# Row sums on ScalarE and a new spread of the fallback's pieces in the first layer of a two-layer kernel

## Chip, cores and metric

One Trainium2 chip, one core of it. The metric is the device time of one launch in microseconds (us). The kernel takes all inputs from HBM and writes the final activations there; float32 throughout, apart from one table of masks.

## The reference

The input `x` has 16 sequences of 256 tokens, 128 features each (4096 tokens). Four blocks follow one another, each as `x = x + block(layernorm(x))`:

```
x = x + L0_attn(layernorm(x))   # linear attention: 32 heads of 4, a decaying state per head, two decays, then an own norm
x = x + L0_ffn(layernorm(x))    # 8 experts, each token to its two best, 1280 places an expert; a dense "fallback" FFN
x = x + L1_attn(layernorm(x))   # gated decay scan
x = x + L1_ffn(layernorm(x))    # two transformer layers with a local window
```

What the change touches lies between the first two. `layernorm` is the usual one,

```
m = mean(x, -1);  v = var(x, -1);  (x - m) / sqrt(v + 1e-5)
```

and the rows that it gives go to the experts and to the fallback network, `gelu(h @ fw1 + fb1) @ fw2 + fb2` with 512 hidden units, whose result stands for a token that an expert had to turn away.

## The kernel before, in words

The 4096 tokens are cut into 8 blocks of 512 (`NB`, `BW`). The first layer is one loop over `t` from -2 to 7 (L796), written out by hand as a software pipeline: in pass `t`, block `t` is scanned, block `t+1` is projected and prepared, block `t-1` is closed, and block `t-2` is normalised for the experts. `do(1, "weigh", cc)` means: step `weigh` of block `t+1`. Each engine runs its instructions in the order in which the loop records them, so a waiting instruction holds up all that stands behind it on its engine. Nothing reorders them.

What one pass does, in the order of the code:

- VectorE (DVE) scans `s` for the two denominators (L505, `s<-beta,phik`). These two scans start a pass in what follows.
- `rotate` for `k` and then for `q` (L448): two projections on TensorE (PE) into PSUM banks `pp`, two products on VectorE, one sum on GpSimd (POOL).
- `add`, `gather`, `den`, `project`, `gates` (PE, with copies on ScalarE, ACT), `share` (a reciprocal on VectorE and a product on POOL), `query`.
- `measure_z`, `sp.sqrt()` and `sp.scales()`: means, variances and scales for the attention's own norm of block `t-1`, and in the same call for the experts' norm of block `t-2`; a `Spread` object has 8 places for them, 0 to 3 for `z` and 4 to 7 for `x`.
- `raised`, `rows_z`, `rows_x`, `rows_n` on ACT; `product`, `shift`, `close` on POOL.
- `value 0` and `value 1` (PE), then `spread_beta 0` (PE, four matmuls into a bank `beta`), `add` of the first decay (PE, `y`), and four rounds of scan, `weigh` (VectorE, `kv<-phik,pp`, reads the bank of `value`) and further `value`s. Between them `turn` (PE `ht`, ACT `hT`), `turn_n` (PE `nt`, ACT `u`) and `logits` (PE `pl`, ACT `lg`).
- `measure_n` (L568): four `bn_stats` and four `bn_aggr` on VectorE over the rows of block `t-1`, which POOL has just finished (L565).
- `spread_beta 1` (PE).

The projections, the transposes, the logits and the fallback's first matmuls share one pool of three PSUM banks (`pp`, L296), which go round in the order of the requests: a matmul into a bank waits until the bank's last reader is done.

Two things run beside. `Route(0, 8)` in pass 4 and `Route(8, 20)` in pass 7 choose experts and places for tokens; their steps are taken one by one with `tick()`, and are mostly small VectorE instructions with a few matmuls (`rt`). And `fallback()` (L731) is cut into pieces, taken with `fill(n)`: for each block, four pieces `inward` (one matmul of 512 columns into a bank `fh`, then one gelu on ACT, L742) and four pieces `outward` (four matmuls of 128 columns each into a bank `fo`; the last one's copy `u<-fo` on ACT, L752). Three blocks (`EARLY`) are done inside the loop, two more after it. Before the change passes 5, 6 and 7 take eight pieces each: two after `rotate k`, two after `rotate q`, four after `value 1`.

[...]

Of the kernel before, what the change touches and what calls it, by code (L numbers as in the profile page):

```python
# [13 lines left out]
AF = mybir.ActivationFunctionType  # L14
ALU = mybir.AluOpType
# [6 lines left out]
D = 128  # L22
# [3 lines left out]
NB = TOK // BW  # L26
LN_EPS = 1e-5
# [8 lines left out]
NIC = INTER // P  # L36
# [99 lines left out]
def tile_kernel(ctx: ExitStack, tc: tile.TileContext, i: dict, out: bass.AP, last: int = 4):  # L136
    nc = tc.nc
    pe, dve, act, pool = nc.tensor, nc.vector, nc.scalar, nc.gpsimd
# [21 lines left out]
    x = const.tile([P, NT, D], F32, name="x")  # L160
# [74 lines left out]
    eps = const.tile([P, 1], F32, name="eps")  # L235
# [57 lines left out]
    with ExitStack() as c:  # L293
# [15 lines left out]
        def turned(name, n=P):  # L309
            t = pp.tile([P, BW], F32, tag="pp", name="wtr")  # L310
            pe.transpose(t[:, :n], nat[name], ident[:n, :n])
            return t[:, :n]

        for name, key in (("L0_attn_Wk", "k"), ("L0_attn_Wq", "q")):
            t = turned(name)
# [7 lines left out]
        t = turned("L0_attn_Wbeta", 2 * NH0).rearrange("p (h m) -> p m h", m=2)  # L323
        act.copy(wz[:, 0:2, :], t)
        t = turned("L0_attn_Wmix", 2 * NH0)
# [3 lines left out]
        t = turned("L0_attn_Wv").rearrange("p (h c) -> p h c", c=HD0)  # L329
# [16 lines left out]
        t = pp.tile([P, BW], F32, tag="pp", name="btr")  # L346
# [18 lines left out]
        class Spread:  # L365


            def __init__(self):
                self.mv = wk.tile([P, 8, 2], F32, tag="mv", name="mv", bufs=3)
                self.lo, self.hi = 8, 0  # L370

            def take(self, at, *parts):
                stats(self.mv, at, *parts)
                self.lo, self.hi = min(self.lo, at), max(self.hi, at + 1)

            def sqrt(self):
                if self.lo > self.hi:
                    return
                self.rs = wk.tile([P, 8], F32, tag="rs", name="rs", bufs=3)
                self.nm = wk.tile([P, 8], F32, tag="nm", name="nm", bufs=3)  # L380
                self.w = slice(self.lo, self.hi)
                act.activation(self.rs[:, self.w], self.mv[:, self.w, 1], AF.Sqrt, bias=eps)

            def scales(self):
                if self.lo > self.hi:
# [5 lines left out]
            def powered(self):  # L391

                if self.lo > self.hi:
                    return
                self.rs = wk.tile([P, 8], F32, tag="rs", name="rs", bufs=3)
                self.nm = wk.tile([P, 8], F32, tag="nm", name="nm", bufs=3)
                w = slice(self.lo, self.hi)
                dve.tensor_scalar(self.rs[:, w], self.mv[:, w, 1], LN_EPS, None, ALU.add)
                pool.tensor_tensor(self.rs[:, w], self.rs[:, w], mhalf0.to_broadcast([P, self.hi - self.lo]), ALU.pow)
                dve.scalar_tensor_tensor(self.nm[:, w], self.mv[:, w, 0], -1.0, self.rs[:, w], ALU.mult, ALU.mult)  # L400

# [19 lines left out]
        class Linear:  # L421
# [144 lines left out]


            def measure_n(self, sp):  # L568
                for j in range(4):
                    sp.take(4 + j, x[:, 4 * self.b + j, :])  # L570

# [202 lines left out]
        EARLY, LATE = 3, 5  # L774
        fall = fallback()

        def fill(n=1):
            for _ in range(n):
                next(fall, None)
# [5 lines left out]
        def tick(most=1):  # L785

            for _ in range(most):
# [3 lines left out]
                if not work:  # L791
                    return

        with tc.manual_schedule():
            later = Spread()
            for t in range(-2, NB):  # L796
                def do(ahead, step, *a):
                    if 0 <= t + ahead < NB:
                        getattr(blocks[t + ahead], step)(*a)

                sp, later = later, Spread()
                if t == 4:
                    work.append(Route(0, 8).steps())
                elif t == 7:
                    work.append(Route(8, 20).steps())
                early = NB - EARLY <= t
                do(0, "scan", 0, HD0)
                do(0, "scan", 1, HD0)
                tick()
                do(0, "product", 0, HD0)  # L810
                do(0, "product", 1, HD0)
                if t == -2:
                    measure_x(0)
                    center_x(0)
                elif t in (0, 1):
                    measure_x(2 * t + 4, 2 * t + 5)
                tick()
                do(1, "rotate", "k")
                if early:
                    fill(2)  # L820
                tick()
                for cc in range(HD0):
                    do(-1, "add", 1, cc)
                do(-1, "gather")
                do(1, "rotate", "q")
                if early:
                    fill(2)
                tick()
                do(0, "den")
                do(-1, "project")  # L830
                do(1, "gates")
                do(0, "share")
                tick()
                do(-1, "measure_z", sp)
                sp.sqrt()
                do(0, "scan", 0, 0)
                tick()
                do(0, "query", 0)
                do(0, "query", 1)
                tick()  # L840
                sp.scales()
                do(1, "raised", "k")
                do(1, "raised", "q")
                if t == -1:
                    measure_x(2, 3)
                do(-1, "rows_z", sp)
                do(2, "rows_x")
                do(-2, "rows_n", sp)
                if t == -2:
                    measure_x(1)  # L850
                    center_x(1)
                elif t in (0, 1):
                    center_x(2 * t + 4, 2 * t + 5)
                for cc in range(HD0):
                    do(0, "product", 0, cc)
                    if cc + 1 < HD0:
                        do(0, "scan", 0, cc + 1)
                        tick()
                    if cc == 1:
                        do(1, "clip")  # L860
                do(-1, "shift")
                do(-1, "close")
                do(1, "feature", "k")
                tick()
                do(1, "value", 0)
                do(1, "value", 1)
                if early:
                    fill(4)
                do(1, "spread_beta", 0)
                for cc in range(HD0):  # L870
                    do(0, "scan", 1, cc)
                    tick()
                    do(1, "weigh", cc)
                    if cc == 0:

                        for c2 in range(HD0):
                            do(0, "add", 0, c2)
                    if cc + 2 < HD0:
                        do(1, "value", cc + 2)
                    if cc == 1:  # L880
                        do(1, "feature", "q")
                        do(2, "turn")
                        do(-2, "turn_n")
                        if t == 1:
                            prepare()
                    if cc == 2:
                        do(-2, "logits")
                    do(0, "product", 1, cc)
                do(-1, "measure_n", later)
                do(1, "spread_beta", 1)  # L890
                if t == -1:
                    center_x(2, 3)


            last_b, prior = blocks[NB - 1], blocks[NB - 2]

            def both(most):
                for _ in range(most):
                    tick()
                    fill()  # L900

            sp, later = later, Spread()
            last_b.shift()
            tick(2)
            for cc in range(HD0):
                last_b.add(1, cc)
            last_b.gather()
            both(2)
            last_b.project()
            both(2)  # L910
            last_b.measure_z(sp)
            sp.powered()
            both(1)
            last_b.rows_z(sp)
            prior.rows_n(sp)
            last_b.close(dve)
            both(1)
            prior.turn_n()
            last_b.measure_n(later)
            later.powered()  # L920
            both(2)
            prior.logits()
            last_b.rows_n(later)
            both(2)
            last_b.turn_n()
            both(2)
# [10 lines left out]
    with ExitStack() as c:  # L937
        dw = c.enter_context(tc.tile_pool(name="d_w", bufs=1))
        ap = c.enter_context(tc.tile_pool(name="d_big", bufs=1))
        early = c.enter_context(tc.tile_pool(name="d_early", bufs=2))  # L940
# [38 lines left out]
        hTs, kTs, vs_, sums, norms = {}, {}, {}, {}, {}  # L979
# [853 lines left out]
```

## Time and profile before

| | |
|---|---|
| three runs | 1410.6, 1418.5, 1419.98 us; median 1418.5 us |
| the profiled execution | 1417.82 us, of which the span from the first to the last instruction is 1415.9 us |
| busy in the span | PE 1215.0 us, DVE 1012.8 us, ACT 782.1 us, POOL 842.6 us |
| pass 2 (91.5 to 118.0 us) | 26.5 us |
| pass 3 (118.0 to 145.5 us) | 27.5 us |
| pass 4, with Route(0, 8) (145.5 to 190.2 us) | 44.7 us |
| pass 5 (190.2 to 221.4 us) | 31.2 us |
| pass 6 (221.4 to 252.6 us) | 31.2 us |
| pass 7, with Route(8, 20) (from 252.6 us) | some 44 us |

Passes are told apart by the start of their two scans `s<-beta,phik`. Times inside the span count from its first instruction. In the views, "idle before" is the time in which an engine had nothing to do ahead of an instruction, with the instruction that ended it; a name such as `L141` is the line of the kernel that issued the instruction (L141 is the helper `mm`, so PE's matmuls are told apart by their tiles).

### The profile page before, as it was taken

How to read it: one execution, taken by the hardware profiler on the slowest of the kernel's cores; microseconds unless marked ns; L12 is line 12 of the kernel's file. 1: busy time of each engine (PE TensorE's matmuls, PEld its weight loads, DVE VectorE, ACT ScalarE, POOL GpSimd, SP SyncE). 2: the span in 40 equal slices, each digit the busy share in tenths (PEclk: the TensorE clock that was granted, in tenths of full speed). 3: DMA queues.
4: the chain of work that ended last, by engine and by line, in shares of the span. 5: the costliest groups of instructions: out<-in, count | busy, mean ns of one | idle time of the engine just before them, and what ended most of it. 6: DMA issues, size and time to landing. Idle time of an engine off the chain costs nothing.

```text
span 1415.9 us, 27034 instructions
## 1 busy us (share of the span) xinstructions
PE 1215.0 (86%) x10101; PEld 843.1 (60%) x10101; DVE 1012.8 (72%) x2426; ACT 782.1 (55%) x1542; POOL 842.6 (60%) x840
## 2 busy tenths in 40 slices
PE   6778599676779978886898998998999999999996
PEld 3344365455557656653566666666676777777774
DVE  5899988765322321377799887888889888988862
ACT  3255345212123433443677777777687787787763
POOL 2667646330543453265789777777678777777521
PEclk9898899777689998996999999999999999999999
DMA  8100000000123142102111111111111111111110
GB/s 246 29 1 15 8 1 16 8 1 15 36 76 88 53 51 54 32 23 66 43 30 38 35 31 29 28 33 35 26 36 26 33 38 26 43 28 26 44 29 25
DMA packets 62171, 53.13 MB, mean 38 GB/s; under 512 B 17001, under 2 KB 49498, under 8 KB 62042
## 3 DMA queue, kind: packets, MB, share of 16 engines
q1 hardware_dynamic: 56925, 40.76, 11.2%
q0 software_dynamic: 4608, 9.45, 3.2%
q8 instruction: 80, 1.31, 0.4%
q10 hardware_dynamic: 509, 1.21, 0.2%
q14 instruction: 49, 0.40, 0.1%
HBM read 21.90 MB, written 10.35 MB: 23 GB/s over the span
## 4 chain that ended last, share of the span: by engine, by line
PE 53%; DVE 27%; ACT 7%; issue 6%; POOL 4%; DMA 2%; another core or an unknown queue 1%; ACTq 0%; SPq 0%; POOLq 0%; DVEq 0%
PE pm L141 19%; PE S L141 8%; PE pq L141 8%; DVE s L505 5%; PE pm L1336 3%; PE pp L141 2%; PE rt L141 2%; PE pm L1291 2%; DVE bnst L259 2%; PE po L141 2%; DVE ss L1238 1%; DVE rot L1237 1%; DVE ex L1325 1%; PE pm L1358 1%
## 5 line engine op out<-in xcount | busy, mean ns | idle before, releaser
L1240 POOL TENSOR_TENSOR t<-t,tabs 128x512 f32<-128x512 f32 x116 | 148.6, 1281 | 68.9 <-ACT t L1236 68.8
L1242 POOL TENSOR_TENSOR rot<-rot,t 128x512 f32<-128x512 f32 x128 | 162.9, 1273 | 19.8 <-DVE rot L1237 10.8
L1280 POOL TENSOR_TENSOR rot<-rot,rn 128x512 f32<-128x512 f32 x128 | 130.8, 1043 | 30.0 <-DVE rc L1352 20.0
L1087 ACT ACTIVATE eh<-S,b1c 128x512 f32<-128x512 f32 (+1 forms) x108 | 66.6, 625 | 145.7 <-PE S L141 103.6
L1338 ACT COPY pT<-pm 128x512 f32<-128x512 f32 x128 | 69.5, 587 | 118.7 <-PE pm L1336 115.7
L1068 POOL DMA_INDIRECT xe<-hd,source x80 | 80.4, 1005 | 88.3 <-ACT c_o L1029 41.6
L141 PE MATMUL pq<-wqkv,hT 128*128 128x512 f32 x256 | 127.7, 621 | 3.8 <-DVE rot L1237 3.4
L509 POOL TENSOR_TENSOR s<-s,q 128x512 f32<-128x512 f32 x64 | 83.7, 1321 | 64.0 <-DVE q L530 32.1
L141 PEld LDWEIGHTS pm<-w,eh 128*128 128x128 f32 x640 | 87.3, 201 | 30.3 <-issue 28.0
L141 PE MATMUL S<-xT,w 128*128 128x512 f32 (+1 forms) x192 | 91.8, 579 | 12.6 <-ACT eh L1087 9.6
L1324 DVE TENSOR_REDUCE ng<-S 128x4 f32<-128x512 f32 x128 | 87.1, 681 | 11.8 <-PE S L141 6.6
L1237 DVE TENSOR_TENSOR rot<-pq,tabs 128x512 f32<-128x512 f32 x128 | 87.3, 682 | 10.1 <-ACT t L1236 9.7
L1401 POOL DMA_INDIRECT g<-ys,outof x64 | 65.5, 1023 | 48.4 <-issue 35.0
L1325 DVE TENSOR_TENSOR ex<-S,ng 128x512 f32<-128x512 f32 x128 | 88.5, 691 | 4.6
L1228 ACT ACTIVATE sq<-pq 128x512 f32<-128x512 f32 x128 | 77.5, 607 | 23.4 <-PE pq L141 14.7
L141 PE MATMUL pm<-w,eh 128*128 128x128 f32 x640 | 88.0, 284 | 2.2 <-issue 2.2
L141 PEld LDWEIGHTS pm<-vs,pT 128*64 128x64 f32 x1024 | 64.8, 137 | 36.4 <-issue 11.9
L1238 DVE TENSOR_REDUCE ss<-sq 128x8 f32<-128x512 f32 x128 | 86.4, 675 | 0.0
L141 PEld LDWEIGHTS pm<-wo,oT 128*128 128x128 f32 x512 | 65.1, 191 | 28.4 <-ACT oT L1360 21.9
L141 PE MATMUL pm<-vs,pT 128*64 128x65 f32 x1024 | 74.1, 225 | 6.5 <-ACT v L1268 3.9
L1336 PE MATMUL pm<-cf,ex 128*128 128x128 f32 x512 | 72.3, 280 | 7.9 <-DVE hid L1557 4.5
L505 DVE TENSOR_TENSOR_SCAN s<-beta,kv 128x512 f32<-128x512 f32 x64 | 76.7, 1205 | 0.0
(333 smaller groups left out, 3247.0 us busy)
## 6 DMA issues: line engine op xcount, KB each, us to landing
vs<-v SPq DMA_DIRECT2D x128, 130.0 KB
w<-in_L_ffn_W_dram SPq DMA_DIRECT2D x16, 256.0 KB
ys<-ye SPq DMA_DIRECT2D x16, 256.0 KB
x<-in_L_attn_x_dram SPq DMA_DIRECT2D x8, 256.0 KB
hd<-hn SPq DMA_DIRECT2D x8, 256.0 KB
up<-u SPq DMA_DIRECT2D x32, 56.0 KB
out_dram<-x SPq DMA_DIRECT2D x7, 256.0 KB
wqkv<-in_L_ffn_wqkv_dram SPq DMA_DIRECT2D x2, 768.0 KB
```

The costliest lines, as they stand in the source:

```text
L141: pe.matmul(o, lhsT, rhs, start=start, stop=stop)
L505: dve.tensor_tensor_scan(s, self.beta[m], a, 0.0, ALU.mult, ALU.add)
L509: pool.tensor_tensor(s, s, self.f["q"] if cc == HD0 else self.q[m], ALU.mult)
L1068: pool.indirect_dma_start(out=self.xe[:, j, :], out_offset=None, in_=hd, in_offset=bass.IndirectOffsetOnAxis(ap=source[:, at_ : at_ + 1], ...
L1237: dve.tensor_tensor(heads(rot[:, k, :]), heads(ps), wide(tabs[l][:, 2 * k, a, :]), ALU.mult)
L1238: dve.tensor_reduce(ss[:, j, k, :], heads(sq), AX.X, ALU.add)
L1240: pool.tensor_tensor(heads(t2), heads(t2), swapped, ALU.mult)
L1242: pool.tensor_tensor(halves(rot[:, k, :]), halves(rot[:, k, :]), halves(t2)[:, :, ::-1, :], ALU.add)
L1280: pool.tensor_tensor(ro, ro, rn, ALU.mult)
L1324: dve.tensor_reduce(ng[:, q, :], self.S[q], AX.X, ALU.max, negate=True)
L1325: dve.tensor_tensor(ex[:, q], self.S[q], ng[:, q, :].unsqueeze(2).to_broadcast([P, 4, P]), ALU.add)
L1336: pe.transpose(ps[:, hp * P : (hp + 1) * P], self.ex[:, q, hp, :], ident)
```

## The change

Two edits in the first layer.

1. `measure_n` of blocks 0 to 6 no longer uses VectorE. ScalarE goes over the four tiles of 128 rows twice, with its accumulator: once as `Identity` with scale 1/128, whose sum over the row is the mean, and once as `Square` of mean minus row, whose sum is 128 times the variance. The elementwise results go into `self.o`, which is no longer needed. Block 7, after the loop, keeps `bn_stats`. Because places 4 to 7 now hold a sum and not a variance, the square root is taken in two ScalarE instructions instead of one, the second with scale 1/128; the form without square root, after the loop, gets a second VectorE instruction in the same way.
2. The 24 pieces of the fallback that the loop takes are spread over passes 3 to 7 by a table. The numbers are pieces after `rotate k`, after `rotate q` and after `value 1`.

```diff
+            def sums(self, junk, rows):
+                self.summed = True
+                self.lo, self.hi = min(self.lo, 4), 8
+                for j, a in enumerate(rows):
+                    act.activation(junk[:, j, :], a, AF.Identity, scale=1.0 / D, accum_out=self.mv[:, 4 + j, 0:1])
+                for j, a in enumerate(rows):
+                    act.activation(
+                        junk[:, j, :], a, AF.Square, bias=self.mv[:, 4 + j, 0:1], scale=-1.0,
+                        accum_out=self.mv[:, 4 + j, 1:2],
+                    )
...
-                act.activation(self.rs[:, self.w], self.mv[:, self.w, 1], AF.Sqrt, bias=eps)
+                mid = 4 if self.summed else self.hi
+                for lo, hi, share in ((self.lo, mid, 1.0), (mid, self.hi, 1.0 / D)):
+                    if lo < hi:
+                        act.activation(self.rs[:, lo:hi], self.mv[:, lo:hi, 1], AF.Sqrt, bias=eps, scale=share)
...
             def measure_n(self, sp):
+                if self.b < NB - 1:
+                    sp.sums(self.o, [x[:, 4 * self.b + j, :] for j in range(4)])
+                    return
                 for j in range(4):
                     sp.take(4 + j, x[:, 4 * self.b + j, :])
...
+        pieces = {3: (1, 1, 2), 4: (0, 0, 4), 5: (1, 1, 2), 6: (0, 0, 5), 7: (1, 1, 5)}
...
-                early = NB - EARLY <= t
+                early = pieces.get(t, (0, 0, 0))
...
                 do(1, "rotate", "k")
-                if early:
-                    fill(2)
+                fill(early[0])
...
                 do(1, "rotate", "q")
-                if early:
-                    fill(2)
+                fill(early[1])
...
                 do(1, "value", 0)
                 do(1, "value", 1)
-                if early:
-                    fill(4)
+                fill(early[2])
                 do(1, "spread_beta", 0)
```

With the table, block 0's four `inward` fall into pass 3 (one, one and two), its four `outward` into pass 4; block 1's four `inward` into pass 5 (one, one and two), its `outward` into pass 6, followed there by block 2's first `inward`; pass 7 takes block 2's other three (one, one, and one after `value 1`) and its `outward`.

In the built program the order of everything else on PE, ACT, DVE and POOL is as before. The eight new ScalarE instructions stand after the copy `lg` (L590) and ahead of the gelus of the next pass and of the copy `ys` (L540).

More of the change, by code (lines that the diff above doesn't have):

```diff
@@ L369, in __init__ @@
                 self.mv = wk.tile([P, 8, 2], F32, tag="mv", name="mv", bufs=3)
-                self.lo, self.hi = 8, 0
+                self.lo, self.hi, self.summed = 8, 0, False
             def take(self, at, *parts):
@@ L397, in powered @@
                 w = slice(self.lo, self.hi)
-                dve.tensor_scalar(self.rs[:, w], self.mv[:, w, 1], LN_EPS, None, ALU.add)
+                mid = 4 if self.summed else self.hi
+                dve.tensor_scalar(self.rs[:, self.lo : mid], self.mv[:, self.lo : mid, 1], LN_EPS, None, ALU.add)
+                if mid < self.hi:
+                    dve.tensor_scalar(self.rs[:, mid:], self.mv[:, mid:, 1], 1.0 / D, LN_EPS, ALU.mult, ALU.add)
                 pool.tensor_tensor(self.rs[:, w], self.rs[:, w], mhalf0.to_broadcast([P, self.hi - self.lo]), ALU.pow)
@@ L792, in tick @@
                     return
+        pieces = {3: (1, 1, 2), 4: (0, 0, 4), 5: (1, 1, 2), 6: (0, 0, 5), 7: (1, 1, 5)}
+        assert NB == 8 and EARLY * 2 * NIC == sum(map(sum, pieces.values()))
         with tc.manual_schedule():
```

## The prediction

> **What bounds it now.** I read first the table of the six passes that the change touches, then the chain of waits inside them, then the idle notes in the timeline. First three passes of the table (time in the stretch, then busy us and instruction counts of PE, weight loads, VectorE, ScalarE, POOL, PE's granted clock, DMA share, GB/s):
>
> ```profile
> 118.00:145.50 27.50, 22.61 (x141) 13.01 (x140) 24.79 (x44) 13.86 (x30) 20.37 (x19) 0.88 0.04 10
> 145.50:190.20 44.70, 28.33 (x175) 18.57 (x174) 42.29 (x84) 14.17 (x31) 22.60 (x20) 0.81 0.02 7
> 190.20:221.40 31.20, 28.24 (x178) 16.39 (x177) 24.83 (x44) 18.00 (x37) 19.32 (x18) 1.00 0.03 9
> ```
>
> VectorE has the largest share in passes 3 and 4, PE in 5. ScalarE is free half the time. That seems to say: unload VectorE. The chain of waits (start, length, what) says it place by place:
>
> ```profile
> 114.75 0.45 PE ht L439 x4
> 115.22 0.59 ACT hT L441
> 115.81 0.50 ACT u L584
> 116.35 1.06 PE pl L141 x8
> 117.41 0.99 PE beta L141 x8
> 118.40 1.72 PE pp L141 x4
> 120.12 1.00 PE y L141 x8
> 121.12 1.91 PE pp L141 x4
> 123.03 0.57 PE den L141 x16
> ...
> 192.36 1.92 PE fh L141 x4
> ...
> 197.19 1.72 PE fh L141 x4
> ...
> 223.84 1.72 PE fh L141 x4
> ...
> 228.47 1.72 PE fh L141 x4
> ```
>
> From one pass to the next the chain runs over PE and ScalarE's copies, not over the statistics: between passes 2 and 3 they are nowhere on it. VectorE waits instead, here in pass 5:
>
> ```profile
> 196.37 0.69 DVE L451 TENSOR_TENSOR t<-pp,cfa 128x512 f32<-128x512 f32 x1 [2.67 <-PE pp L141]
> ...
> 200.06 1.75 DVE L520 RECIPROCAL rd<-rd 128x256 f32<-128x256 f32 x1 [2.14 <-ACT rd L517]
> ```
>
> Last, PE before `beta` in passes 3 and 5 in the timeline, and then the clock of PE in pass 3, in slices of 4 us with the columns of the first table:
>
> ```profile
> 135.42 2.05 PE L141 MATMUL beta<-bt,cfa 128*128 128x128 f32 x8 [4.17 <-DVE s L505]
> ...
> 211.30 1.13 PE L141 MATMUL beta<-bt,cfa 128*128 128x128 f32 x8 [0.60 <-DVE s L505]
> ```
> ```profile
> 136.00:140.00 4.00, 4.00 (x16) 2.02 (x16) 4.00 (x6) 3.12 (x9) 3.98 (x3) 0.50 0.00 0
> 140.00:144.00 4.00, 3.28 (x15) 1.72 (x13) 4.00 (x6) 1.08 (x2) 3.94 (x3) 0.88 0.24 66
> ```
>
> After 4.17 us without work PE runs at half clock until about 140.9, some 5.5 us after it resumes (0.88 of a slice of 4 us means that 0.96 us of it were slow). In pass 5 the sixteen `fo` matmuls fill that gap, and `beta` takes 1.13 instead of 2.05.
>
> **1. Statistics off VectorE.** A block's eight instructions take 1.6 us of its time (143.87 to 145.47). What each boundary returns:
>
> - Passes 1/2: PE ends `q` 0.2 before VectorE wants it. -0.2.
> - 2/3, 4/5, 5/6: PE's chain `pl`, `beta`, `k`, `kr`, `y`, `q` decides when the next product can start; VectorE's waits in front of `q` (0.73 in pass 3, 2.67 and 2.80 in 5 and 6) only grow by 1.6. 0.
> - 3/4: the first scan can move up by 1.6, the second waits for `beta`, ready at 145.8, and starts then instead of at 146.6. -0.8.
> - 6/7: counted with pass 6 below.
> - End of pass 7: the four rows' statistics stand in the Route chain (294.98 to 296.58). PE's `rt` waits 3.12 us for VectorE after them, but part of that is used up by the gelu and `fh` that now precede `fo` (fh at half clock 1.7). -1.0, between -1.6 and 0.
>
> The second square root stands in the chain (`ACT rs L382`) in passes 2, 3, 5 and 6: about 0.2 each, by the start of the next instruction 0.21 after the first (130.68, 130.89). +0.8. In 4 and 7 Route covers it.
>
> The eight sums are not in the trace. Below: four `hn` rows of the same size take 1.66 us, 0.40 each from start to start. Above: nothing overlapped, 0.498 for one, plus 0.30 for writing a small result (L382): 0.80. I take 0.45, nearer to the `hn` rows, as the operation is the same. They start after `lg` (117.63 in pass 3) and last 3.6; behind them in ScalarE's queue stand a table load (1.28), the first gelu (0.69) and `ys`. The gelu frees the bank of the second `fh`, which PE reaches at 122.96 + 0.86 = 123.8; 117.63 + 3.6 + 1.28 + 0.69 = 123.2. Hidden, by 0.6. `ys` is needed by `po` at 124.9 without pieces, later with them. Cost 0; if the cover is gone, see the rival.
>
> **2. Pieces after `rotate`.** Two `fh` stand on the chain with 1.72 us (the first pair of pass 5 with 1.92), 0.86 each. Pass 3 gets two: +1.72. Pass 5 loses two: -1.82. Pass 6 loses four: -3.44. Pass 7 loses two off the chain (PE waits 2.51 for VectorE's `els` after them): 0. Sum -3.54.
>
> **3. Pieces after `value 1`.** Here is the cost. Banks `pp` go round in threes, and the program's order shows for passes 3 and 5: the third `fh` takes the bank of `query 1`, the fourth takes that of `value 0`, which VectorE frees with its first `kv` (ends 138.10 in pass 3). Behind the waiting matmul stand `beta`, `y` and `value 2`, which ran before that point or right at it; VectorE's third `kv` waits for `value 2`. In pass 3 it started at 141.58, 3.48 after the first `kv`. Now, counted from the end of the first `kv`: PE has idled some 6 us, so half clock for 5.5 us: `fh` 1.74 (as `value` at 177.42, 3.47 for two), `beta` 2.05, and 1.7 us of `y`'s 2.09; the rest of `y` 0.2, `value 2` 0.95: ready at 6.65, 3.2 late. `value 3` 0.95 and `ht` 0.45 follow, so `nt` starts at 8.05 instead of 4.31 (142.41): **+3.7** in pass 3. In pass 5 `pl` starts 1.33 after `nt` (as 142.41 to 143.74), at 9.4 instead of 6.08 (220.07 against 213.99): **+3.3**. At full clock throughout (0.86 + 0.99 + 1.0 + 0.95 = 3.8) these are 0.9 and 0.45.
>
> [...]
>
> In pass 6 one `fh` follows the `fo` pieces and waits for the first `kv` likewise, after 3.3 us of idling (241.97 to 245.27), so I take half clock again. `value 2` at 6.65, `value 3` 7.6, `nt` 8.05, `pl` 8.9, `beta` from 9.85 to 10.9 (without `ht`, as there is no block 8). The second scan of pass 7 started 8.5 after that `kv` and now waits for `beta`: **+2.4**, VectorE's 1.6 being lost in this. At full clock: -0.5.
>
> In pass 4 the sixteen `fo` matmuls are new after `value 1`, which ends at 180.7. PE then works without a gap through `beta`, `rt`, `y`, `value 2`, `rt`, `value 3`, `ht`, `nt` to `pl`, and VectorE waits for `rt` already (0.18). 3.73 us as in pass 5 (206.96), 0.6 more while the clock is still half, less 0.5 because `beta` then runs at full clock: **+3.8**, between 3.2 (full clock) and 5.9 (half clock, as at 286.66). `fo` was hidden in passes 5 and 6, so nothing is won by its leaving.
>
> **Sum.** -0.2 -0.8 -1.0 +0.8 -3.54 +3.7 +3.3 +2.4 +3.8 = +8.5. The profiled execution took 1417.8 us (span 1415.9 and 1.9 around it), 0.05% below the median of 1418.5: 1417.8 + 8.5 = **1426.3 us**. What follows the first layer starts later by the same and is not changed.
>
> **The rivals.**
>
> *The clock holds.* The half clock is what makes the blocked `fh` dear. If PE stays at full clock (its idle time is cut in two by the third `fh`), the three bold terms of passes 3, 5 and 6 become 0.9, 0.45 and -0.5: sum -0.1, 1417.7 us. Against it: the granted clock fell after every gap of over 4 us in passes 2 to 4. 17%.
>
> *VectorE is the bound after all.* Its busy share of 90% and more in passes 2 to 4 speaks for it. If the next pass really starts when VectorE is free, and the blocked matmuls are covered as `fo` is today, all seven blocks return 1.6 (-11.2), the pieces -3.5, the square roots +0.8: -13.9, 1403.9 us. Against: VectorE's idle notes and the chain. This is the case in which it gets faster. 11%.
>
> *ScalarE becomes late.* If a sum takes over 0.53 us each, the gelu comes after 123.8 and the second `fh`, `den` and all behind wait in passes 3 and 5. At 0.80: 6.4 + 1.28 + 0.69 after 117.63 is 126.0, 2.2 late, twice: 1430.7. At 1.0 it would be 3.8 twice, and `ys` 1.3 late for `po` in three other passes: 1437.8. For it: no accumulating instruction is in the trace, and the margin is 0.6. 12%.
>
> **How the numbers follow.** The forecast has 60%: its own range, by the bounds of `fo`, the end of pass 7 and a gap that halves the clock only in part, is 1420 to 1430. The range for 8 in 10 reaches down over the clock's rival into VectorE's and up into ScalarE's: 1412 to 1433. About 1% (14 us) is what a measurement of this kernel tells from no change. Faster by more than that (below 1404.3) is half of VectorE's rival: 6%. Slower (above 1432.7): most of ScalarE's case above 0.9 us and a tail of the forecast, 10%. Within 1%: 84%.
>
> **What would show it.** Right: passes 3 to 7 last some 32.3, 48.5, 32.9, 30.4 and 43 us; VectorE waits some 3 us for PE before the third `kv` in passes 3 and 5; PE's `beta` takes 2.05 in pass 5; the granted clock of pass 5 falls below 1.00; sums of 0.4 to 0.5 us from start to start; `bnst<-x` gone from VectorE and its idle time up by about as much. Wrong: no wait before that `kv`, pass 3 no longer than 29.5, or the first gelus of passes 3 and 5 starting over 6 us after `lg`.

## The result, and the profile after

Over 20 runs of each, the changed kernel takes 1422.05 us at the median and the kernel before 1417.81 us; the ratio is 1.0027, 95% interval 1.0017 to 1.0038. That is some 3.8 us slower (2.4 to 5.4), where 8.5 were forecast: the right direction, less than half the size. The time itself lies inside the forecast's own range of 1420 to 1430 us. In what follows, times in "us against before" are such ratios times 1418.

The profiled execution of the changed kernel took 1418.93 us, its span 1417.2 us, which is only 1.3 us more than before. But up to the first scan of pass 1 the two programs differ in nothing, and there this execution happened to be 5.2 us quicker (56.28 us against 61.50). From that scan to the gated product `o` after the loop it took 263.59 us, before 258.72: the first layer lost 4.9 us. A second profile of the same kernel (after_again below) gives 262.76 us. I compare this stretch, and the passes in it, rather than spans.

First the passes of the changed kernel, from second scan to second scan (time in the stretch, then busy us and instruction counts of PE, weight loads, VectorE, ScalarE, POOL, PE's granted clock, DMA share, GB/s); passes 3, 4 and 5:

```profile
113.77:146.16 32.39, 25.49 (x147) 14.21 (x146) 23.51 (x35) 21.72 (x55) 21.55 (x20) 0.89 0.03 9
146.16:193.63 47.47, 31.65 (x207) 22.00 (x206) 41.02 (x75) 17.29 (x50) 21.46 (x20) 0.82 0.02 6
193.63:225.41 31.78, 24.88 (x147) 14.10 (x146) 23.50 (x35) 21.73 (x55) 20.60 (x19) 0.89 0.03 9
```

VectorE has 1.3 us less to do in each pass than the 24.8 of before in passes 3 and 5, and passes 3 and 4 are longer nevertheless. Pass 5 now has a clock of 0.89 where it had 1.00. The chain of waits through the end of pass 3 shows what took VectorE's place:

```profile
135.26 2.08 PE fh L141 x2
137.34 1.71 PE beta L141 x8
...
145.06 1.01 PE beta L141 x8
...
146.16 1.22 DVE s L523
```

From the end of the first `kv` (135.2) to the second scan of the next pass (146.16) nothing but PE and the copies of its results on ScalarE is on it. At its head stands the blocked `fh`, the fourth, which waits for the bank that the first `kv` frees. VectorE, which decided this stretch before, is not there. Before, the chain of the same stretch was a row of scans and `kv` products on VectorE. Its end, with the eight statistics instructions, from 143.87 on, between the two lines:

```profile
143.37 0.58 DVE kv L500
...
145.55 2.22 DVE s L505 x2
```

The waits of VectorE that hang on the blocked `fh`, from the timeline, before the third `kv` of passes 3, 5 and 6 (in pass 3 of the kernel before, VectorE did not wait there):

```profile
141.58 0.69 DVE L518 TENSOR_TENSOR kv<-phik,pp 128x512 f32<-128x512 f32 x1 [2.82 <-PE pp L141]
...
220.83 0.69 DVE L518 TENSOR_TENSOR kv<-phik,pp 128x512 f32<-128x512 f32 x1 [2.20 <-PE pp L141]
...
250.91 0.69 DVE L518 TENSOR_TENSOR kv<-phik,pp 128x512 f32<-128x512 f32 x1 [2.21 <-PE pp L141]
```

And PE in pass 5, the blocked matmul and what follows it:

```profile
215.13 2.08 PE L141 MATMUL fh<-u,fw 128*128 128x512 f32 x2 [6.18 <-DVE kv L518]
217.00 1.74 PE L141 MATMUL beta<-bt,cfa 128*128 128x128 f32 x8
```

At full clock this one `fh` (two instructions) takes 1.02 us, as at 128.07 in pass 3, and `beta` 1.06, as at 184.15 in pass 4. Slices of 4 us in passes 3 and 5 say when the clock comes back (columns as above, the clock is the third from the end):

```profile
136.00:140.00 4.00, 4.00 (x18) 2.16 (x16) 2.76 (x4) 2.77 (x4) 3.92 (x4) 0.51 0.23 66
216.00:220.00 4.00, 4.00 (x19) 2.34 (x18) 2.63 (x4) 2.64 (x4) 3.92 (x4) 0.70 0.24 66
```

A mean of 0.51 means that all but 0.1 us of the slice ran at half: it ended at 139.9, 4.7 us after `fh` began. 0.70 means 2.4 us at half: it ended at 218.4, 3.3 us after.

In pass 4 the `fo` matmuls stand ahead of everything that follows (PE, then VectorE's wait for the routing's product):

```profile
180.29 4.02 PE L141 MATMUL fo<-fw,fh 128*128 128x128 f32 x32
184.15 1.06 PE L141 MATMUL beta<-bt,cfa 128*128 128x128 f32 x8
```
```profile
189.03 0.26 DVE L751 TENSOR_TENSOR table<-table,rt 128x96 f32<-128x96 f32 x1 [3.45 <-PE rt L141]
```

Before, `beta` began right after `value` and took 1.64 us at part clock, and VectorE's wait there was 0.18:

```profile
186.13 0.25 DVE L729 TENSOR_TENSOR table<-table,rt 128x96 f32<-128x96 f32 x1 [0.18 <-PE rt L141]
```

Last, the sums on ScalarE. Each is two instructions, the pass over the row and the reading of the accumulator, and they overlap in part:

```profile
112.79 0.31 ACT L381 ACTIVATE o<-x 128x128 f32<-128x128 f32 x1
113.00 0.19 ACT L381 ACTIVATION_READ_ACCUMULATOR o<-x 128x1 f32 x1
```

The eight run from 112.79 to 115.61: 2.8 us, by the starts 0.29 for a mean and 0.385 for a square. After a load of ScalarE's function table (`ACT_TABLE_LOAD`, 1.28 us) the first gelu follows at 116.92. It ends at 117.61, well ahead of the second `fh` at 118.98.

### The profile page after: what moved, and what is told of

The parts are those of the page before. It is cut to its first block, busy times and chain, and to the rows that moved or that the text cites. A ratio compares the mean times of both kernels' runs of the same rounds, so it can differ in the third digit from the quotient of the medians.

```text
span 1417.2 us, 27098 instructions
## 1 busy us (share of the span) xinstructions
PE 1206.9 (85%) x10101; PEld 839.9 (59%) x10101; DVE 1005.4 (71%) x2371; ACT 802.5 (57%) x1662; POOL 843.6 (60%) x840
## 4 chain that ended last, share of the span: by engine, by line
PE 56%; DVE 22%; ACT 8%; issue 6%; POOL 4%; another core or an unknown queue 1%; DMA 1%; ACTq 0%; SPq 0%; POOLq 0%; DVEq 0%
PE pm L141 19%; PE S L141 8%; PE pq L141 8%; PE pm L1359 3%; DVE s L523 3%; PE pp L141 3%; PE rt L141 2%; PE pm L1314 2%; PE po L141 2%; DVE bnst L259 1%; PE beta L141 1%; DVE ss L1261 1%; DVE rot L1260 1%; PE pm L1381 1%
## 5 line engine op out<-in xcount | busy, mean ns | idle before, releaser
L527 POOL TENSOR_TENSOR s<-s,q 128x512 f32<-128x512 f32 x64 | 83.9, 1322 | 68.1 <-DVE s L523 31.5
L141 PEld LDWEIGHTS pm<-w,eh 128*128 128x128 f32 x640 | 87.4, 201 | 31.8 <-issue 29.4
```

The lines of the kernel that those rows point to most:

```text
L141: pe.matmul(o, lhsT, rhs, start=start, stop=stop)
L527: pool.tensor_tensor(s, s, self.f["q"] if cc == HD0 else self.q[m], ALU.mult)
```

## The experiments

My theory after the result (A): the sums are a gain of a few us; the new spread loses more, by the blocked fourth `fh` with the half clock behind it, and by `fo` in pass 4. First the whole in one table. Passes are counted from second scan to second scan in one profile of each; "stretch" runs from the first scan of pass 1 to `o`, and "fill" gives the pieces in passes 3, 4, 5, 6, 7 as after `rotate k`, after `rotate q`, after `value 1`.

| kernel | fill | pass 2 | 3 | 4 | 5 | 6 | stretch | ratio to before |
|---|---|---|---|---|---|---|---|---|
| before | 0, 0, 224, 224, 224 | 26.5 | 27.5 | 44.75 | 31.1 | 31.3 | 258.7 | 1 |
| the changed kernel | 112, 004, 112, 005, 115 | 28.0 | 32.4 | 47.5 | 31.8 | 29.7 | 263.6 | 1.0027 |
| after_again | the same | 27.5 | 32.0 | 47.3 | 31.7 | 29.7 | 262.8 | one run |
| sums_only | 0, 0, 224, 224, 224 | 27.6 | 27.5 | 44.5 | 32.3 | 30.1 | 256.3 | 0.9978 |
| spread_only | 112, 004, 112, 005, 115 | 26.6 | 31.6 | 47.6 | 31.4 | 30.0 | 264.7 | 1.0051 |
| keep_warm | as changed, PE kept busy | 27.5 | 30.3 | 46.2 | 30.3 | 28.0 | 258.5 | 1.0011 |
| own_bank | as changed, blocked `fh` in another bank | 27.5 | 32.5 | 47.2 | 32.9 | 27.6 | 261.8 | 1.0012 |
| none_behind | 220, 004, 220, 004, 224 | 27.5 | 30.9 | 47.8 | 30.9 | 26.7 | 258.2 | 1.0002 |
| one_behind | 211, 004, 211, 004, 224 | 27.6 | 31.8 | 47.3 | 34.0 | 27.2 | 262.2 | 1.0033 |
| one_aside | 211, 004, 211, 004, 224, one `fh` in another bank | 27.8 | 31.2 | 46.3 | 30.4 | 28.4 | 259.3 | 0.9991 |
| fo_out_of_4 | 112, 0, 004, 224, 224 | 27.5 | 32.0 | 43.8 | 28.0 | 30.1 | 255.8 | 0.9961 |
| gap4 | 0, 8 in the gap, 0, 224, 224 | 27.5 | 27.5 | 44.3 | 27.5 | 30.1 | 251.3 | 0.9920 |

Where nothing differs, passes repeat within 0.5 us (pass 2 of the kernels with the sums, pass 6 with 224 and the sums), and pass 4 within 1.6 us (46.2 to 47.8 with `fo`, 43.8 to 44.75 without). Differences under that are not read. Two places are worse: pass 6 with 004 and the sums takes 26.7, 27.2 and 28.4 us, and pass 1, which is not in the table, takes 28.4 us in all kernels with the sums but 31.5 in the profile of one_aside, whose stretch is too long by as much.

**sums_only**: edit 1 alone, that is the changed kernel with the pieces where they were.

```diff
-        pieces = {3: (1, 1, 2), 4: (0, 0, 4), 5: (1, 1, 2), 6: (0, 0, 5), 7: (1, 1, 5)}
+        pieces = {5: (2, 2, 4), 6: (2, 2, 4), 7: (2, 2, 4)}
```

> The row sums on ScalarE alone, with the fallback's pieces where they were (2, 2 and 4 in passes 5, 6, 7). Theory A (VectorE's statistics are mostly covered by PE's chain from pass to pass): it gains only at the boundary 3/4 (some 0.6 us), at 6/7 (1.6) and at the end of pass 7 (about 1), pays 0.65 for the second square root: 2 to 4 us faster than before. Rival B (VectorE is the bound of the loop): 7 x 1.6 us come off, some 10 us faster. Rival C (the sums make ScalarE late): slower than before by 2 us or more.

Measured: ratio 0.9978, interval 0.9965 to 0.9992, so 3.1 us faster (1.1 to 5.0). Edit 1 is a gain, and neither the 10 us that a bound by VectorE would give nor a late ScalarE is seen. VectorE at the head of pass 3 of this kernel shows what limits it:

```profile
119.02 1.22 DVE L523 TENSOR_TENSOR_SCAN s<-beta,phik 128x512 f32<-128x512 f32 x1 [0.79 <-PE beta L141]
```

The first scan now comes right behind the last `kv`, at 117.01, and the second waits for `beta`: of the 1.6 us that the statistics free, 0.8 are lost again at once, and 0.6 more in VectorE's next wait for PE, ahead of `q` (1.30 us against 0.73 before). Pass 3 is 27.5 us long with and without the sums. By the stretch the gain is 2.4 us, of which 0.6 by the end of pass 2, 1.2 in pass 6 and 1.6 after it; pass 5 was 1.1 longer in this profile.

**spread_only**: edit 2 alone, with `measure_n` on VectorE as before.

```diff
             def measure_n(self, sp):
-                if self.b < NB - 1:
-                    sp.sums(self.o, [x[:, 4 * self.b + j, :] for j in range(4)])
-                    return
```

> The new places of the fallback's pieces alone, with the statistics on VectorE as before. Theory A: all of the loss comes from here, the fourth inward matmul waiting for a bank in passes 3, 5 and 6 and the outward ones of pass 4: 5 to 8 us slower than before, 1 to 3 us slower than the changed kernel. Rival B: over 10 us slower than the changed kernel, as the statistics are back. Rival C: as fast as before or faster.

Measured: ratio 1.0051 (1.0031 to 1.0071), 7.2 us slower (4.4 to 10.1), where 5 to 8 were expected. With -3.1 for the sums the two parts make +4.1; both together measured +3.8. They add up.

**keep_warm**: the changed kernel with PE given extra work in the hole.

```diff
                 t = bank("fh")
+                for _ in range(6 if b < 2 and ci == 2 else 0):
+                    mm(t, fw1[:, ci * P : (ci + 1) * P], cols_n(b))
                 mm(t, fw1[:, ci * P : (ci + 1) * P], cols_n(b))
...
                 t = hid[b, "o"]
+                for _ in range(3 if b == 1 and j == 0 else 0):
+                    mm(t, fw1[:, 0:P], hid[b][0])
```

> The changed kernel with extra matmuls that change no result: six more into the bank of the third inward matmul in passes 3 and 5 (5.2 us of PE's 6.2 us gap) and three into the bank of the outward ones in pass 6 (2.6 of 3.5 us). The fourth inward matmul waits for its bank as before, but PE meets it at full clock. Theory A (half clock makes the blocked matmul dear): the wait before VectorE's third kv shrinks from 2.8, 2.2 and 2.2 us to under 1, and the kernel is 4 to 6 us faster than the changed one, near the kernel before. Rival D (the wait for the bank is the price, whatever the clock): within 1.5 us of the changed kernel.

Measured: ratio 1.0011 (0.9995 to 1.0026), some 2.3 us under the changed kernel, between what the theories gave; its interval overlaps with that of the changed kernel (1.0017 to 1.0038), so the time decides nothing. The passes do. The waits before the third `kv` of passes 3, 5 and 6 are 0.60, 0.61 and 0.60 us, under 1 as theory A had it. PE in pass 3 of this kernel:

```profile
140.00 1.12 PE L141 MATMUL fh<-u,fw 128*128 128x512 f32 x2 [1.04 <-DVE kv L518]
```

The blocked `fh` still waits for `kv`, but now at full clock (granted 1.00 from 136 to 144 us), and passes 3, 5 and 6 are 2.1, 1.4 and 1.75 us shorter than in the changed kernel. That is the half clock's share in the three blocked matmuls, 5.2 us in all, by one profile of each kernel.

**own_bank**: the changed kernel with the three blocked `fh` (pass 3, 5 and 6) in the PSUM bank of the routing, which is free then.

```diff
-                t = bank("fh")
+                aside = (b, ci) in ((0, 3), (1, 3), (2, 0))
+                t = pr.tile([P, BW], F32, tag="rt", name="fh") if aside else bank("fh")
```

> The changed kernel with the blocked inward matmul (the fourth of passes 3 and 5, the one of pass 6) in a PSUM bank of its own, that of the Route step, which is free in these passes; so beta and y no longer stand behind a wait for VectorE's first kv. PE still idles and meets beta at half clock. Theory A: no wait before the third kv, some 8 us faster than the changed kernel and 2 to 5 us faster than the kernel before. Rival E (half clock alone, without the wait for the bank, costs the time): it stays within 2 us of the changed kernel.

Measured: ratio 1.0012 (0.9992 to 1.0033). I expected 8 us less than the changed kernel and got 2: the expectation fell, and the time is near that of rival E (half clock alone). Pass 3 is as long as ever (32.5), though no `kv` waits. PE in pass 3, and the second scan of VectorE after it:

```profile
142.80 0.63 PE L457 MATMUL ht<-cf,h 128*128 128x128 f32 x4 [1.29 <-DVE kv L518]
144.51 0.63 PE L605 MATMUL nt<-cf,hn 128*128 128x128 f32 x4 [1.08 <-DVE kv L518]
```
```profile
149.57 1.22 DVE L523 TENSOR_TENSOR_SCAN s<-beta,phik 128x512 f32<-128x512 f32 x1 [4.07 <-PE beta L141]
```

The wait has moved. In the built program of the changed kernel, `ht` takes the bank of the fourth `fh` and waits for its gelu; with that `fh` elsewhere `ht` takes the bank of `value 2` and `nt` that of `value 3`, which VectorE frees only with its third and fourth `kv`. (So the three banks do not go round strictly by the order of the requests, as I had described them: the bank of the third `fh`, freed late by ScalarE, is passed over twice.) PE idles there, falls to half clock (its next `pl` and `beta` take 1.74 and 2.06 us, at full clock 1.06 and 1.14), and the scan waits 4.07 us. Some 1.6 of these are the half clock of rival E, 0.8 stand there in sums_only too, and the rest are the waits for banks. New theory (W): behind `value 1` the bank is what costs; any `fh` there hands the wait on.

**none_behind**: both `fh` of passes 3 and 5 behind a `rotate`, none behind `value 1`; pass 6 has its four `fo` alone, pass 7 is as before.

```diff
-        pieces = {3: (1, 1, 2), 4: (0, 0, 4), 5: (1, 1, 2), 6: (0, 0, 5), 7: (1, 1, 5)}
+        pieces = {3: (2, 2, 0), 4: (0, 0, 4), 5: (2, 2, 0), 6: (0, 0, 4), 7: (2, 2, 4)}
```

> The changed kernel with the two fh products that passes 3 and 5 issue behind value 1 moved in front, two behind each rotate: pieces {3: (2, 2, 0), 4: (0, 0, 4), 5: (2, 2, 0), 6: (0, 0, 4), 7: (2, 2, 4)}. The PSUM ring behind value 1 then has the requests of before. Theory A (the loss of passes 3 and 5 is TensorE's wait for a bank behind value 1 and the half clock after it; a product behind a rotate costs 0.86 us and nothing else): pass 3 by second scans takes 27.5 + 3.44 = 30.9 us against 32.39 in the changed kernel, no wait of over 1 us before a kv; the kernel lands 3 to 6 us under the changed one, 2.5 us under to 1 us over the kernel before. Rival B (the clock drops in that hole anyway, whether something is queued there or not): the half clock follows value 1 as before, the gain is under 1.5 us against the changed kernel, that is 2 to 4 us over before.

Measured: ratio 1.0002 (0.9986 to 1.0018), 3.5 us under the changed kernel. Pass 3:

```profile
117.06:147.98 30.92, 25.80 (x147) 14.28 (x146) 23.42 (x35) 20.64 (x54) 20.33 (x19) 0.89 0.03 10
```

Passes 3 and 5 are 3.44 longer than the 27.48 of sums_only's pass 3: four products at 0.86 and nothing else. The clock is 0.89 as in the changed kernel, so PE slows down here too (its `beta` takes 2.04 in pass 3), but VectorE waits for it nowhere in pass 3 for more than 0.9 us ahead of a `kv` or a scan. Against this kernel the blocked `fh` cost the changed one 3.2, 2.6 and 3.1 us in passes 3, 5 and 6 (lengths less two or four products at 0.86: 32.39 - 1.72 against 30.92 - 3.44, 31.78 - 1.72 against 30.91 - 3.44, 29.73 against 26.65). The 3.1 of pass 6 rests on this kernel alone: one_behind and one_aside, with the same pieces in pass 6, took 27.2 and 28.4 there. And pass 4 keeps its 3 us: they belong to `fo`.

**one_behind**: one `fh` of passes 3 and 5 behind `value 1`, two behind `rotate k`.

```diff
-        pieces = {3: (1, 1, 2), 4: (0, 0, 4), 5: (1, 1, 2), 6: (0, 0, 5), 7: (1, 1, 5)}
+        pieces = {3: (2, 1, 1), 4: (0, 0, 4), 5: (2, 1, 1), 6: (0, 0, 4), 7: (2, 2, 4)}
```

> The changed kernel with one fh behind value 1 in passes 3 and 5 and two behind rotate k: pieces {3: (2, 1, 1), 4: (0, 0, 4), 5: (2, 1, 1), 6: (0, 0, 4), 7: (2, 2, 4)}. Nothing waits for a bank behind value 1, but the program then gives ht the bank of value 2 and nt that of value 3, as in own_bank. Theory W (with three banks a product behind value 1 only hands its wait on: TensorE now stands before ht and nt for the third and fourth kv, idles, and runs logits and beta at half clock): no wait before the third kv, but 3 to 4 us before the second phik scan in passes 3 and 5; pass 3 stays at 31.5 to 33.5 us and the kernel 1 to 4 us over before, as own_bank's 1.7. Theory A in its simple form (the blocked product itself is the loss): pass 3 takes 29.5 to 30.5 us and the kernel lands 1 to 4 us under before.

Measured: ratio 1.0033 (1.0019 to 1.0047), the slowest of the moved ones, though no product waits behind `value 1`. VectorE at the second scans of passes 4 and 6:

```profile
150.04 1.22 DVE L523 TENSOR_TENSOR_SCAN s<-beta,phik 128x512 f32<-128x512 f32 x1 [2.47 <-PE beta L141]
...
231.32 1.22 DVE L523 TENSOR_TENSOR_SCAN s<-beta,phik 128x512 f32<-128x512 f32 x1 [4.66 <-PE beta L141]
```

W's place is right, and so is its length of pass 3 (31.8). The waits, 2.5 and 4.7, lie on either side of the 3 to 4 that it gave, and the kernel is 4.7 us over before where it had 1 to 4. In the first case `pl` and `beta` took 1.06 and 1.14 us, where own_bank, with its wait of 4.07, had 1.74 and 2.06: the wait of 2.5 came without half clock in these two.

**one_aside**: the same, with that one `fh` in the routing's bank.

```diff
-                t = bank("fh")
+                aside = (b, ci) in ((0, 3), (1, 3))
+                t = pr.tile([P, BW], F32, tag="rt", name="fh") if aside else bank("fh")
```

> one_behind once more, with the one fh product that passes 3 and 5 issue behind value 1 written into the routing's PSUM bank (pool a_pr, free in these passes) and not into the three banks that the values and transposes share. Nothing else differs from one_behind; the requests to the three banks are those of none_behind. Theory W (behind value 1 it is the bank that costs, not TensorE's time: the product itself runs in TensorE's idle time there): no wait before ht and nt beyond sums_only's, no wait of over 1.3 us before the second phik scan; passes 3 and 5 at 27.5 + 3 x 0.86 = 30.1 us (one_behind: 31.8 and 33.9); the kernel 3 to 6 us under one_behind and 0.5 to 3 us under none_behind, that is 1 to 3 us under before. Rival T (a product behind value 1 costs TensorE's time and clock there, in whatever bank): passes 3 and 5 stay at 31 us or more and the kernel within 1.5 us of one_behind, 3 to 6 us over before.

Measured: ratio 0.9991 (0.9976 to 1.0005), 6 us under one_behind by the change of a bank alone: rival T is out by the time and by pass 5, which is 30.4, near the 30.1 expected. Pass 3 is 31.2 and not 30.1, which alone would fit T, and there the second scan waits 1.89 us. PE in that pass:

```profile
143.66 0.63 PE L605 MATMUL nt<-cf,hn 128*128 128x128 f32 x4 [1.05 <-DVE kv L518]
...
146.26 1.89 PE L141 MATMUL beta<-bt,cfa 128*128 128x128 f32 x8
```

PE had its clock back at 139.6 (0.88 in the half us from 139.5, 1.00 after it) and so was ahead of VectorE: it idled for 1.05 before `nt` and 1.09 before `pl`. The granted clock was 1.00 from 142 to 146, but the `beta` on the path took 1.89 us from 146.26, where one_behind's took 1.14: by its length, an estimate, most of it ran at half clock.

**fo_out_of_4**: nothing in pass 4; block 0's `fo` behind `value 1` of pass 5, blocks 1 and 2 in passes 6 and 7.

```diff
-        pieces = {3: (1, 1, 2), 4: (0, 0, 4), 5: (1, 1, 2), 6: (0, 0, 5), 7: (1, 1, 5)}
+        pieces = {3: (1, 1, 2), 5: (0, 0, 4), 6: (2, 2, 4), 7: (2, 2, 4)}
```

> The changed kernel with no fill in pass 4: block 0's fo products run behind value 1 of pass 5, blocks 1 and 2 in passes 6 and 7 as before: pieces {3: (1, 1, 2), 5: (0, 0, 4), 6: (2, 2, 4), 7: (2, 2, 4)}. Theory A (16 fo products stand on the path in pass 4, where VectorE waits for the routing's products behind them, and beside other work in pass 5): pass 4 back from 47.5 to 44.5 to 45 us, pass 5 under 29.5 us since its four fh products are gone, pass 3 still 32 to 32.6; the kernel 4 to 6 us under the changed one, about 0 to 2 us under before. Rival F (fo costs its 3.3 us in whatever pass it stands): pass 5 stays at 31 to 32 us, and the kernel lands 1 to 3 us over before.

Measured: ratio 0.9961 (0.9947 to 0.9976), 5.5 us under before (3.4 to 7.5); I expected 0 to 2. The stretch is 2.9 shorter. Pass 4 is back at 43.8, pass 3 keeps its 32.0 with the blocked `fh`, and pass 5, with sixteen `fo` matmuls and no `fh`, takes 28.0, only 0.5 more than 27.5 without any piece. So `fo` costs 0.5 us in pass 5 and some 3 in pass 4; rival F is out.

**gap4**: a version meant to win. In the chain of pass 4 PE waits 11.5 us for the routing's masks. All eight pieces of block 0 go there.

```diff
-        pieces = {3: (1, 1, 2), 4: (0, 0, 4), 5: (1, 1, 2), 6: (0, 0, 5), 7: (1, 1, 5)}
+        pieces = {6: (2, 2, 4), 7: (2, 2, 4)}
...
                 do(0, "query", 1)
+                fill(4 if t == 4 else 0)
...
                 do(-2, "rows_n", sp)
+                fill(4 if t == 4 else 0)
```

> A version meant to beat both: the sums on ScalarE, all eight pieces of block 0 in pass 4 right behind the two query steps, where TensorE waits 11.5 us for the routing's masks (four fh behind query 1, their four fo behind the rows), nothing in passes 3 and 5, passes 6 and 7 as before. Theory A (pieces cost nothing in a hole of TensorE that is longer than they are, 0.86 us behind a rotate): pass 4 at 44.5 to 45.5 us, pass 5 3.4 to 5 us shorter than in sums_only's 32.3; the kernel 5 to 9 us under before, 2 to 6 us under sums_only. Rival L (the four gelu and the table load before them push ScalarE's phi, rows and h late, or the pieces hold up the routing's products): pass 4 grows by 3 us or more and the kernel is no faster than sums_only, at 1414 us or above.

Measured: ratio 0.9920 (0.9893 to 0.9947), 11 us under before (7.5 to 15.2; 7.3 by the medians, 1410.91 against 1418.18 us), where 5 to 9 were expected, and faster than both kernels. PE in pass 4:

```profile
157.39 3.87 PE L141 MATMUL fh<-u,fw 128*128 128x512 f32 x8
161.09 4.11 PE L141 MATMUL fo<-fw,fh 128*128 128x128 f32 x32
169.12 1.52 PE L141 MATMUL rt<-at,one 128*128 128x96 f32 x8 [3.92 <-DVE at L742]
```

Eight us of pieces, and `rt` still waits 3.92 for VectorE: they are free here, although the four `fh` and their `fo` all take banks of the pool of three (in the loop `fo` comes from that pool too, which the list of its users ahead of the prediction leaves out). Pass 4 is 44.3, pass 5 27.5.

**after_again**: the changed kernel once more, for a second profile.

> The changed kernel unaltered, for one more profile. It shows how much of a pass's length is the place of the half clock in that one execution. Theory A: passes 3 to 6 within 0.7 us of 32.4, 47.5, 31.8 and 29.7, the waits before the third kv in passes 3, 5 and 6 again 2 to 3 us, and the half clock after TensorE resumes 3 to 5 us long. Rival: the forecast's 5.5 us is as common, then one of the three reaches it and its pass is 1 us longer.

Measured, as theory A had it: passes 3 to 6 of 32.0, 47.3, 31.7 and 29.7 us, waits before the third `kv` of 2.46, 2.11 and 2.22. In slices of half a us the half clock ends 4.0, 3.1 and 3.8 us after PE resumes. None reaches 5.5.

## Why the prediction was right and wrong

*Direction, places and the chain of waits: right.* VectorE's bound was not what set the pass (sums_only gained 3 us, not 11); pieces behind a `rotate` cost 0.86 each (none_behind, to 0.01); the fourth `fh` waits for the first `kv`, and its wait returns before the third; the half clock follows; `fo` is dear in pass 4 and almost free in 5. Of the marks that were to show it, the waits (2.8 and 2.2 for some 3 us), the clock under 1.00 in pass 5 and the vanished `bnst<-x` came. `beta` of pass 5 took 1.74 and not 2.05, and the sums 0.29 to 0.385 and not 0.4 to 0.5.

*The terms, against the profile before* (lengths of the stretches between second scans):

| | forecast | profile after |
|---|---|---|
| pass 3 | +4.8 | +4.9 |
| pass 4 | +3.8 | +2.7 |
| pass 5 | +1.7 | +0.6 |
| pass 6 | -0.8 | -1.55 |
| from there to `o` | -1.0 | -1.7 |

The rest of the stretch, the boundary 1/2 with pass 2, is nothing in the forecast (-0.2 and a second square root) and -0.1 in the profile: +8.5 against +4.9 in all. That pass 3 agrees to 0.1 is luck in part: its blocked `fh` cost 0.5 us less than forecast, and the 0.8 that its end was to return did not come in it.

*The step that failed* is the price of the blocked matmul, the three bold terms of part 3: +3.7, +3.3, +2.4. From the end of the first `kv` to `pl` pass 3 lost 3.2 (8.79 against 5.64) and pass 5 2.1 (8.17 against 6.08); from that `kv` to the second scan pass 6 lost 1.5 (10.00 against 8.48). That is 2.6 of the 3.6 us by which the sum exceeds the stretch. The number behind it is "PE has idled some 6 us, so half clock for 5.5 us", and the 5.5 come from a single row, in which PE had idled 4.17 us. After the blocked `fh` the half clock ended 4.7, 3.3 and 4.0 us after PE resumed in this profile, 4.0, 3.1 and 3.8 in the second, and 3.8, 3.0 and 3.9 in spread_only.

The granted clock shows why the row does not carry over. First a slice of pass 3 before, then slices of passes 3 and 5 of the changed kernel (the clock is the third from the end):

```profile
132.00:136.00 4.00, 0.58 (x3) 0.61 (x4) 4.00 (x5) 3.96 (x9) 2.87 (x5) 0.76 0.00 0
...
132.00:136.00 4.00, 0.73 (x1) 0.50 (x2) 4.00 (x5) 4.00 (x12) 4.00 (x4) 0.64 0.00 0
...
208.00:212.00 4.00, 0.95 (x3) 0.12 (x1) 3.95 (x6) 3.94 (x7) 2.16 (x5) 0.95 0.00 0
```

They mean 1.9, 2.9 and 0.4 us at half: the clock fell at 134.1, 133.1 and 211.6. It came back, by the later slices, at 140.9, 139.9 and 218.4. So the half clock lasted 6.8 us each time, and part of it passed while PE still idled: 1.3 us in the row, 2.2 and 3.5 ahead of the blocked `fh`. The longer idle stretch uses up more of it. Where PE resumed with `beta` after 4.2 to 4.3 us, the half clock went on for 4.8 to 6.3 us (passes 1 to 3 of the kernel before, 1 and 2 of the changed one, 3 of none_behind: six cases, mean 5.5); where a blocked `fh` followed 6.0 to 6.2 us, it went on for 3.0 to 4.7 us (passes 3 and 5 of the changed kernel, after_again and spread_only: six cases, mean 3.6). In pass 6 PE had idled for 3.5 us only; there the clock fell 0.5 us after PE resumed, at 245.7, and was back 3.4 us later, at 249.1.

The six changes of the clock around the three blocked `fh` of the changed kernel (133.1, 139.9, 211.6, 218.4, 245.7 and 249.1) lie 6.8, 71.7, 6.8, 27.3 and 3.4 us apart, in this trace 2, 21, 2, 8 and 1 times 3.41 us. What sets these moments was not shown.

none_behind and keep_warm measure the same term without the kernel before. In none_behind pass 6 keeps the 1.6 us that VectorE saves, and the forecast's +2.4 had that lost, so against it the three terms read 3.7, 3.3 and 4.0. Measured are 3.2, 2.6 and 3.1, or 2.1 less. Of this the half clock (the changed kernel less keep_warm) is 2.1, 1.4 and 1.75, where the forecast, as the difference between its terms with and without half clock, had 2.8, 2.85 and 2.9: 3.3 too much. What remains at full clock is 1.1, 1.15 and 1.3, where it had 0.9, 0.45 and 1.1: 1.1 too little, most of it in pass 5. So the half clock is the term that was too large, and a smaller miss the other way hid part of it.

*Smaller ones.* `fo` in pass 4: forecast 3.8, the way from `value 1` on lengthened by 3.3; of the "0.6 more while the clock is still half" 0.3 came (`fo` took 4.02 and not 3.73), as the clock was back at 180.9, 0.6 us after `fo` began, and the shorter way of VectorE behind it, without the statistics, gave 0.6 back. The end of pass 7: -1.0 taken, -1.7 measured, -1.6 in sums_only; the forecast's lower bound of -1.6 was the better guess, as the time that it gave to the gelu and `fh` ahead of `fo` was not lost. The second square root and the 0.8 of the boundary 3/4: pass 3, which was to show both, is 27.5 us long in sums_only and before. Up to the second scan of pass 4 sums_only is 0.5 us ahead, where the forecast had 0.6, but it has them by the end of pass 2 already. In the sum the two terms cancel.

*The rivals.* The clock does not hold: every blocked `fh` of the changed kernel ran into half clock (2.08, 2.08 and 1.57 us, against 1.02 at 128.07). ScalarE is not late: eight sums take 2.8 us and not 3.6, and the margin that was put at 0.6 us is 1.4 in pass 3.

*What stays open.* No run moved the changes of the clock against the work; their place differs from profile to profile (between the changed kernel's two, by 0.7, 0.2 and 0.1 us after PE resumed in passes 3, 5 and 6), so the half clock that a given idle stretch leaves can be forecast as a range only, here 3.0 to 4.7 us behind some 6.1. Behind `value 1`, `fo` also takes one bank of the three and costs 0.5 us in pass 5 of fo_out_of_4, where one `fh` made passes 3 and 5 of one_behind 1.7 and 3.9 us longer than their three products at 0.86 explain; why was not worked out. And keep_warm's time is only 2.3 us under the changed kernel's, where its stretch is 4.3 to 5.1 shorter; the rest of the program, the same in both, ran from 1089.4 to 1101.0 us in the profiles shown here, so one profile cannot tell.

## What to carry to other kernels

Filler belongs where the engine idles for longer than the filler lasts and where the bank that it takes is not missed by the waiting chain behind it. With three banks, one `fh` behind `value 1` only hands its wait on, as own_bank and one_behind show; the same banks cost nothing in the hole of gap4, where all that follows waits longer for something else. Price a blocked matmul with what stands behind it in the queue. Count the half clock from the moment at which it begins (6.8 us from there in passes 3 and 5 of the changed kernel and in pass 3 before) and not from where the work resumes: three rows of the kernel before (4.9, 5.7 and 5.5 us, all after 4.2 us without work) agreed among themselves and still misled, as the new idle stretch was 2 us longer. Of two edits made together, cost and try each alone: here one gained 3 us and the other lost 7; with a better place for the same pieces the two gain 11 by the ratio, 7 by the medians.

## What was not expected of the hardware

- Where the clock fell around an idle stretch of PE of 3.4 to 6.2 us ahead of `beta` or `fh`, the half clock ended between 2.9 us (pass 3 of one_aside, after 3.43 us) and 6.3 us (pass 2 of the changed kernel, after 4.30 us) after work resumed. From its fall to its return it lasted 6.8 us (passes 1 to 3 before; 1, 2, 3 and 5 of the changed kernel) or 3.4 us (pass 6 of the changed kernel, pass 3 of one_aside). At one place of the changed kernel, its two executions differed by 0.1 to 0.7 us in its end.
- The same start-up code reached the first scan of pass 1 anywhere from 56.3 to 62.0 us in the profiles shown here, and this is larger than the effect under study.
- A sum by ScalarE's accumulator costs an instruction of its own, 0.19 us, of which 0.09 shows from start to start: 0.29 us for a row tile with a sum, where four such tiles without (the `hn` rows, which also read a scale and a bias for each row) took 1.65 us, 0.4 each.
